# The causal mask of a first attention, written into PSUM by matmuls of 32 rows instead of 128

## The chip, the cores and the metric

The kernel runs on one core of one Trainium2 chip. The metric is device time in microseconds (us); the time before is 1464.79 us, the median of 3 runs (1464.25 to 1464.92). A profile is one further execution, recorded by the hardware profiler.

## What is computed

One transformer block, on 8 sequences (`B`) of 128 tokens (`S`) of width 512:

```
h  = x @ cond_weight[adapter[b]].T             # a weight per sequence, gathered
q, k, v = h @ wq, h @ wk, h @ wv               # 32 query heads of 16, 8 key heads of 16
scores  = q k^T * 16**-0.5, causal: key <= query, else a very negative number
x1 = x + softmax(scores) v @ wo                # the first attention
y  = second attention of x1: 32 heads of 128, RMS norm, RoPE,
     512 cached keys (gathered pages) and 128 own keys, no causal mask
out = x1 + y @ W + b + low-rank terms per sequence
```

Only the causal line is touched by the change. The kernel adds the mask as numbers: it first writes -1e30 where key > query, and 0 elsewhere, into the PSUM banks, and then lets the matmuls of the scores add to them.

## The kernel before, in words

The order of all work is written out by hand: each engine runs its instructions in program order, and a framework only adds the semaphore waits and the rotation of buffers.

**First attention** (lines 662 to 760). A loop over `k` from 0 to 15 takes two steps per sequence (`b = k // 2`, `hb = k % 2`), each with 16 of the 32 heads; `k` = 16 only finishes. In step `k` TensorE runs `scores1(k)` and then the rest of step `k - 1` and the preparation of the next sequence:

- even `k`: `flip_x1(b - 2)` (L477), `condition(b + 1)` (L489), transposes of the probabilities of `k - 1` (`flip_p`, L606), `project_kv(b + 1)` (L519, L523), more transposes, `values1(k - 1)` (L625).
- odd `k`: `out_proj1(b - 1)` (L641), `flip_p`, `project_q(b + 1)` (L503), `flip_p`, `flip_x(b + 2)` (L477), `values1(k - 1)`.

VectorE follows with the negated maxima (`nm`, L572), copies out of PSUM (L497, L514, L612, L632) and the sums (L595, L596), ScalarE with the exponentials (L586), GpSimd with the division (L597) and the gathers of the condition weights (L296, four DMAs a sequence). `values1` uses 32-column groups of the array (128x32 tiles), the score matmuls 32-row groups, everything else in the loop the full array.

`scores1(k)` fills two PSUM tiles of two banks each, so four banks; bank `j` holds four heads by 128 keys for 128 queries. Before, each bank gets one bf16 matmul (L553): stationary `identb` (a 128x128 identity), moving `causal` (the mask four times side by side, 512 columns). Then eight fp32 score matmuls (L563) add to it, `rr` = 0, 1 and `j` = 0 to 3, bank `j` out of rows 32j to 32j+31 of the array. The profile shows each fp32 matmul as two weight loads and two matmuls, so L563 has 16 of each per step and L553 has 4 of each.

**Setting up** (lines 311 to 327). `identb` is a bf16 copy of `ident` (VectorE, L322); GpSimd makes the 128x128 mask (a memset and an affine select in masks.py), VectorE copies it four times to bf16 (L327). On GpSimd these two stand between `gather_w(1)` and `gather_w(2)`.

**Step 1's extra work.** After `values1` of step 1 (`b == 0`), `indices()` and `angles()` (L350 to L390) run on GpSimd and VectorE: the angles of the second attention's tables.

**Buffers.** `tile_a` takes tiles of tag "a" from a ring of 12. The condition weights `cw` (four tiles a sequence) are its first users, and many tiles of the second attention follow. The scores' PSUM tiles come from a ring of two.

**Second attention** (from L767): 64 units of one key head and one sequence, TensorE almost without a gap. The change does not touch it.

Of the kernel before, what the change touches and what calls it, by code (L numbers as in the profile page):

```python
# [10 lines left out]

F32 = mybir.dt.float32
BF16 = mybir.dt.bfloat16
I32 = mybir.dt.int32
AF = mybir.ActivationFunctionType
ALU = mybir.AluOpType
AX = mybir.AxisListType
PSUM = bass.MemoryType.PSUM

P = 128  # L20
# [8 lines left out]
NEG = -1.0e30  # L29
# [12 lines left out]
def block_kernel(  # L42
# [28 lines left out]
    nc = tc.nc  # L71
# [8 lines left out]
    both = ctx.enter_context(tc.tile_pool(name="both", bufs=2))  # L80
# [5 lines left out]
    def one(shape, dtype, name):  # L86
        return const.tile(shape, dtype, tag=name, name=name)

    def tile_a(shape, name):
        return both.tile(shape, F32, tag="a", name=name, bufs=12)  # L90
# [8 lines left out]
    ident = one([P, P], F32, "ident")  # L99
# [177 lines left out]
    with (  # L277
# [40 lines left out]
        ]  # L318
        for v in vpad:
            nc.vector.memset(v[:], 0.0)  # L320
        identb = p1w.tile([P, P], BF16, tag="identb", name="identb")
        nc.vector.tensor_copy(identb[:], ident[:])  # L322
        causal_f = both.tile([P, P], F32, tag="ka", name="causal_f")
        make_causal_mask(nc, causal_f[:], NEG)
        causal = p1w.tile([P, 4, P], BF16, tag="causal", name="causal")
        for n in range(4):
            nc.vector.tensor_copy(causal[:, n, :], causal_f[:])  # L327

        lens = p1w.tile([P, B], I32, tag="lens", name="lens")
        nc.sync.dma_start(out=lens[:], in_=seqlens.unsqueeze(0).to_broadcast([P, B]))  # L330
# [215 lines left out]
        def scores1(k):  # L546
            b, hb = divmod(k, 2)
            h = H[k]
            h["sc"] = [
                p_sc.tile([P, 2, 4 * S], F32, tag="sc", name=f"sc1_{k}_{n}") for n in range(2)  # L550
            ]
            for j in range(4):
                nc.tensor.matmul(  # L553
                    h["sc"][j // 2][:, j % 2, :],
                    identb[:],
                    causal[:].rearrange("p n t -> p (n t)"),
                    start=True,
                    stop=False,
                )
            for rr in range(2):  # L560
                for j in range(4):
                    rows = slice(32 * j, 32 * j + 32)
                    nc.tensor.matmul(  # L563
                        h["sc"][j // 2][:, j % 2, rr * 2 * S : (rr + 1) * 2 * S],
                        qT[b][rows, 2 * hb + rr, :],
                        kbd[b][rows].rearrange("p h t -> p (h t)"),
                        start=False,
                        stop=(rr == 1),
                    )
            h["nm"] = p1.tile([P, 2, 8], F32, tag="nm1", name=f"nm1_{k}")  # L570
            for n in range(2):
                nc.vector.tensor_reduce(  # L572
                    h["nm"][:, n, :],
                    h["sc"][n][:].rearrange("p j (h t) -> p (j h) t", t=S),
                    AX.X,
                    ALU.max,
                    negate=True,
                )
            h["pr"] = []
# [82 lines left out]
        for k in range(2 * B + 1):  # L662
            b, hb = divmod(k, 2)
            more, now, last = b + 1 < B, k < 2 * B, k - 1
            if now:
                scores1(k)
# [415 lines left out]
```

## Time and profile before

| | us |
|---|---|
| median of 3 runs | 1464.79 |
| the profiled execution, its own time | 1463.75 |
| its span (first to last instruction) | 1462.0 |
| PE (TensorE matmul) busy | 1419.5 |
| VectorE (DVE) busy | 931.6 |
| ScalarE (ACT) busy | 653.3 |
| GpSimd (POOL) busy | 553.9 |
| L553, mask matmuls, 64 of them, busy | 16.6 |
| L563, score matmuls, 256 of them, busy | 18.3 |
| first attention, start to about | 248 |

How to read it: the span is the time of the profiled execution between its first and last instruction; what is around it (1.75 us here) is launch and end. Busy times of an engine merge overlapping instructions. PE rows are matmuls, PEld rows weight loads (they overlap the matmuls); matmuls are pipelined, so an instruction's duration is longer than the distance to the next one, and distances between starts say more than durations. A shape such as 32x128 after an engine's name is rows by columns of the array that the instruction uses. The chain of work goes back from the last instruction, at each step to what released it.

### The profile page before, as it was taken

The page shows a single profiled execution, that of the slowest core. Times are in us where ns is not written, and L with a number is a line of the kernel's source. Part 1 is how long each engine was busy: PE and PEld are TensorE (multiplying, and loading weights), DVE is VectorE, ACT ScalarE, POOL GpSimd, SP SyncE. Part 2 cuts the span into 40 slices and gives each one's busy share as a digit, 9 for nine tenths or more (in the row PEclk, how much of TensorE's full clock was granted, in tenths as well). Part 3 has the DMA queues.
Part 4 walks back from the last instruction along what each step waited for, and adds up shares of the span by engine and source line. Part 5 has one row for each costly group of instructions (what it writes and reads, how often), then busy time and mean ns, then how long its engine had stood idle before and what let it go on. Part 6 is the DMA issues. An engine that isn't in the chain of part 4 may idle for free.

```text
span 1462.0 us, 19888 instructions
## 1 busy us (share of the span) xinstructions
PE 1419.5 (97%) x6064; PEld 911.0 (62%) x6064; DVE 931.6 (64%) x2271; ACT 653.3 (45%) x1513; POOL 553.9 (38%) x542
## 2 busy tenths in 40 slices
PE   6899999899999999999999999999999999999997
PEld 5677765466666666666666666666666666566654
DVE  2766665666666667666666676666677656556552
ACT  2545443444444444444444444444444434434430
POOL 4475352433334333344444343333334332333120
PEclk9999999999999999999999999999999999999999
DMA  5232400444444565444445654444466433443331
GB/s 199 66 109 61 174 31 0 121 128 117 117 115 118 152 189 150 119 119 119 119 120 159 192 155 122 123 119 117 117 175 190 129 108 89 115 116 94 80 94 51
DMA packets 155642, 175.00 MB, mean 120 GB/s; under 512 B 94160, under 2 KB 99536, under 8 KB 155536
## 3 DMA queue, kind: packets, MB, share of 16 engines
q1 hardware_dynamic: 140688, 131.77, 32.4%
q0 software_dynamic: 14848, 41.96, 10.1%
q8 instruction: 49, 0.80, 0.2%
q14 instruction: 57, 0.47, 0.1%
HBM read 71.38 MB, written 2.10 MB: 50 GB/s over the span
## 4 chain that ended last, share of the span: by engine, by line
PE 93%; DVE 2%; SPq 2%; DMA 1%; issue 1%; ACT 1%; POOL 1%; DVEq 0%; POOLq 0%
PE op L886 18%; PE sc L830 15%; PE qp L176 15%; PE yp L905 15%; PE kvp L216 7%; PE sc L837 4%; PE att L641 2%; PE qp L503 2%; PE qTp L253 2%; PE hp L489 2%; PE fp L939 2%; PE pT1p L606 2%; PE o L625 1%; SPq L874 1%; PE sc L563 1%; PE sc L553 1%
## 5 line engine op out<-in xcount | busy, mean ns | idle before, releaser
L843 DVE CUSTOM_DVE_ANT_0 pr<-sc,mask,nq 128x640 f32<-128x640 f32 x256 | 225.8, 883 | 151.3 <-PE sc L837 138.1
L853 ACT ACTIVATE pr<-pr,nm 128x640 f32<-128x640 f32 x256 | 211.8, 827 | 190.9 <-DVE nm L843 188.4
L830 PE MATMUL sc<-kT,qT 128*128 128x512 f32 x512 | 263.3, 596 | 1.5 <-ACT kTo L274 1.5
L176 PE MATMUL qp<-wq,x1T 128*128 128x512 f32 x512 | 251.2, 593 | 0.0
L202 POOL TENSOR_TENSOR qa<-qa,qb 128x512 f32<-128x512 f32 x64 | 81.5, 1274 | 438.4 <-DVE sums L820 438.4
L886 PE MATMUL op<-pT,vg 128*128 128x256 f32 x1024 | 242.2, 379 | 2.6 <-DMA pT<-fl 2.1
L905 PE MATMUL yp<-wo,oT 128*128 128x512 f32 x512 | 230.4, 593 | 1.4 <-DVE oT L894 1.4
L886 PEld LDWEIGHTS op<-pT,vg 128*128 128x128 f32 x1024 | 194.2, 190 | 30.5 <-issue 2.3
L821 ACT ACTIVATE pr<-pr,sums 128x640 f32<-128x640 f32 x256 | 208.4, 814 | 0.0
L824 DVE STREAM_TRANSPOSE fl<-pr 128x640 f32<-128x640 f32 x256 | 192.3, 807 | 1.2 <-DMA pT<-fl 0.7
L837 PEld LDWEIGHTS sc<-kTo,qT 128*128 128x128 f32 x512 | 96.8, 190 | 124.9 <-issue 106.3
L905 PEld LDWEIGHTS yp<-wo,oT 128*128 128x128 f32 x512 | 92.4, 190 | 93.7 <-issue 91.8
L159 POOL DMA_INDIRECT kg<-in_k_cache_dram,idx_kv x128 | 131.9, 1031 | 35.3 <-issue 34.9
L159 POOL DMA_INDIRECT vg<-in_v_cache_dram,idx_kv x128 | 127.8, 999 | 36.7 <-issue 36.7
L830 PEld LDWEIGHTS sc<-kT,qT 128*128 128x128 f32 x512 | 88.1, 192 | 79.4 <-issue 72.9
L255 ACT COPY qT<-qTp 128x512 f32<-128x512 f32 x64 | 37.5, 585 | 205.2 <-PE qTp L253 205.2
L216 PEld LDWEIGHTS kvp<-wkv,x1T 128*128 128x128 f32 x512 | 97.3, 190 | 40.5 <-issue 30.4
L216 PE MATMUL kvp<-wkv,x1T 128*128 128x256 f32 x512 | 120.9, 379 | 0.0
L243 POOL TENSOR_TENSOR rs<-ss,minus_half 128x5 f32<-128x5 f32 x64 | 76.5, 1196 | 81.4 <-DVE ss L241 81.4
L176 PEld LDWEIGHTS qp<-wq,x1T 128*128 128x128 f32 x512 | 82.8, 191 | 31.5 <-issue 31.5
L837 PE MATMUL sc<-kTo,qT 128*128 128x128 f32 x512 | 99.3, 276 | 0.0
L597 POOL TENSOR_TENSOR pr<-pr,sums 128x1024 f32<-128x1024 f32 x32 | 60.1, 1897 | 98.5 <-DVE sums L596 91.9
(136 smaller groups left out, 1669.8 us busy)
## 6 DMA issues: line engine op xcount, KB each, us to landing
pT<-fl SPq DMA_DIRECT2D x1024, 80.0 KB
kT<-flk SPq DMA_DIRECT2D x496, 32.0 KB
wq<-in_wq_dram SPq DMA_DIRECT2D x8, 1024.0 KB
wo<-in_wo_dram SPq DMA_DIRECT2D x8, 1024.0 KB
wkv<-in_wkv_dram SPq DMA_DIRECT2D x8, 512.0 KB
xs<-in_x_dram SPq DMA_DIRECT2D x8, 256.0 KB
kg<-in_k_cache_dram,idx_kv POOLq DMA_INDIRECT x128, 3.6
vg<-in_v_cache_dram,idx_kv POOLq DMA_INDIRECT x128, 3.6
```

The source lines that it names most:

```text
L159: nc.gpsimd.indirect_dma_start(out=dst[:, c].rearrange("p n d -> p (n d)"), out_offset=None, in_=src, in_offset=bass.IndirectOffsetOnAxis( ...
L176: nc.tensor.matmul(s["qp"][:].rearrange("p h d -> p (h d)"), x1T[b][:, c, :], weights[g][0][:, c, :], start=(c == 0), stop=(c == KC - 1),)
L202: nc.gpsimd.tensor_tensor(qa[:], qa[:], qb[:], ALU.add)
L216: nc.tensor.matmul(s["kp"][:], x1T[b][:, c, :], weights[g][1][:, c, :], start=(c == 0), stop=(c == KC - 1))
L821: nc.scalar.activation(prs[r][:], prs[r][:], AF.Copy, scale=sums[:, r : r + 1])
L824: nc.vector.transpose(s["flips"][:, :, :, r, :].rearrange("p b c j -> p c b j"), prs[r][:])
L830: nc.tensor.matmul(sc[:, : NBLK * P].rearrange("p (k j) -> p k j", j=32), s["qT"][:, r, :], s["kT"], start=True, stop=True,)
L837: nc.tensor.matmul(sc[:, NBLK * P : NK], s["qT"][:, r, :], s["kTo"][:], start=True, stop=True)
L843: nc.vector.tensor_tensor_reduce(out=pr[:], in0=sc[:, :NK], in1=mask[:], scale=s["nq"][:, r : r + 1], scalar=3.0e38, op0=ALU.add, op1=ALU.min,
L853: nc.scalar.activation(pr[:], pr[:], AF.Exp, bias=nm[:, r : r + 1], scale=-1.0, accum_out=sums[:, r : r + 1],)
L886: nc.tensor.matmul(ops[h][:, : 2 * S], cached(u, "vg", c) if c < NBLK else s["vo"][:], s["pT"][:, :, c, 2 * h : 2 * h + 2, :].rearrange("p ...
L905: nc.tensor.matmul(yp[:], s["oT"][:, r, :], weights[g][2][:, r, :], start=(r == 0), stop=(r == REP - 1))
```

## The change

The mask is no longer one matmul of 128 rows per bank but four matmuls of 32 rows per bank, one for each block `c` of 32 columns (32 keys), and bank `j` uses the rows 32j to 32j+31 of the array, as the score matmuls do. The stationary operand is now the mask (`causal[rows, c, :]`, 32x128: for key 32c+i and query t, -1e30 where t < 32c+i), the moving operand a 32x32 identity repeated for the four heads (`eye32`, 128 columns). A step has 16 mask matmuls and 16 weight loads in place of 4 and 4; the order is `c` outer, `j` inner. The setting up changes with it:

```diff
-        identb = p1w.tile([P, P], BF16, tag="identb", name="identb")
-        nc.vector.tensor_copy(identb[:], ident[:])
-        causal_f = both.tile([P, P], F32, tag="ka", name="causal_f")
-        make_causal_mask(nc, causal_f[:], NEG)
+        eye_f = p1w.tile([P, 32], F32, tag="eye_f", name="eye_f")
+        nc.vector.tensor_reduce(
+            eye_f[:], ident[:].rearrange("p (n r) -> p r n", r=32), AX.X, ALU.add
+        )
+        eye32 = p1w.tile([P, 4, 32], BF16, tag="eye32", name="eye32")
+        nc.vector.tensor_copy(eye32[:], eye_f[:].unsqueeze(1).to_broadcast([P, 4, 32]))
+        row = p1w.tile([P, 1], I32, tag="row", name="row")
+        for n in range(4):
+            nc.gpsimd.iota(
+                row[32 * n : 32 * n + 32, :], pattern=[[0, 1]], base=0, channel_multiplier=1
+            )
+        row_f = p1w.tile([P, 1], F32, tag="row_f", name="row_f")
+        nc.vector.tensor_copy(row_f[:], row[:])
+        ahead = both.tile([P, 4, P], I32, tag="a", name="ahead", bufs=12)
+        nc.gpsimd.iota(ahead[:], pattern=[[-32, 4], [1, P]], base=0, channel_multiplier=0)
+        ahead_f = tile_a([P, 4, P], "ahead_f")
+        nc.vector.tensor_copy(ahead_f[:], ahead[:])
         causal = p1w.tile([P, 4, P], BF16, tag="causal", name="causal")
-        for n in range(4):
-            nc.vector.tensor_copy(causal[:, n, :], causal_f[:])
+        nc.vector.tensor_scalar(causal[:], ahead_f[:], row_f[:], NEG, ALU.is_lt, ALU.mult)
...
-            for j in range(4):
-                nc.tensor.matmul(
-                    h["sc"][j // 2][:, j % 2, :],
-                    identb[:],
-                    causal[:].rearrange("p n t -> p (n t)"),
-                    start=True,
-                    stop=False,
-                )
+            for c in range(4):
+                for j in range(4):
+                    rows = slice(32 * j, 32 * j + 32)
+                    nc.tensor.matmul(
+                        h["sc"][j // 2][:, j % 2, :].rearrange("p (n t) -> p n t", n=4)[
+                            :, :, 32 * c : 32 * c + 32
+                        ],
+                        causal[rows, c, :],
+                        eye32[rows],
+                        start=(c == 0),
+                        stop=False,
+                    )
```

`ahead` and `ahead_f` are two further tiles of the ring of 12 (tag "a"), taken between `gather_w(1)` and `gather_w(2)`. Nothing else is different.

More of the change, by code (lines that the diff above doesn't have):

```diff
@@ L9 @@
 from concourse._compat import with_exitstack
-from concourse.masks import make_causal_mask, make_identity
+from concourse.masks import make_identity
 F32 = mybir.dt.float32
```

## The prediction

> **What bounds the kernel now.** I read the page's busy times and its chain first, then the chain of work stretch by stretch through the first attention, then single starts of L553 and L563 in narrow windows of the timeline.
>
> ```profile
> PE 1419.5 (97%) x6064; PEld 911.0 (62%) x6064; DVE 931.6 (64%) x2271; ACT 653.3 (45%) x1513; POOL 553.9 (38%) x542
> PE 93%; DVE 2%; SPq 2%; DMA 1%; issue 1%; ACT 1%; POOL 1%; DVEq 0%; POOLq 0%
> ```
>
> TensorE is the bound nearly everywhere. The chain of the stretch 112 to 139 us (start, length, what; steps 7 and 8 begin at 113.50 and 126.39) shows it inside one step:
>
> ```profile
> 113.50 0.97 PE sc L553 x4
> 114.47 1.07 PE sc L563 x16
> 115.54 3.63 PE att L641 x8
> ...
> 124.09 0.59 ACT pT L612
> ...
> 126.39 0.97 PE sc L553 x4
> 127.36 1.08 PE sc L563 x16
> 128.43 0.59 PE x1Tp L477 x4
> ```
>
> The mask and the scores are 0.97 + 1.07 = 2.04 us on the chain, and what follows on TensorE starts at once. It is not so everywhere. The chain of 31 to 66 us, where steps 1 and 2 stand:
>
> ```profile
> 44.36 1.90 POOL pr L597
> 46.26 0.06 POOL iota_s L353
> ...
> 47.91 1.40 DVE ang_f L381 x8
> ...
> 54.39 2.26 DVE nm L572 x2
> 56.65 0.61 DVE hT L497
> 57.30 2.07 PE kvp L519 x8
> ```
>
> Here GpSimd (divisions and gathers back to back from 33.82) and then VectorE's angles decide when TensorE goes on at 57.30; it had been idle for 5.0 us. A TensorE that finishes step 1 or 2 sooner only waits longer.
>
> Single starts, from the timeline (start, length from first start to last end):
>
> ```profile
> 101.73 0.60 PE L553 MATMUL sc<-causal,identb 128*128 128x512 bf16 x2
> ```
> ```profile
> 102.70 0.50 PE L563 MATMUL sc<-kbd,qT 32*128 32x256 f32 x4
> ```
> ```profile
> 102.70 0.31 PEld L563 LDWEIGHTS sc<-kbd,qT 32*128 32x128 f32 x8 [0.42 <-issue]
> ```
>
> One L553 takes 379 ns, so the second starts 0.60 - 0.38 = 0.22 after the first: 512 bf16 columns cost 0.216 us each. One L563 of this first round takes 478 ns, so four of them in 0.50 start within 22 ns: the four groups of rows work at once, and even the loads of the next round overlap. The four rounds lie 0.216 apart.
>
> **TensorE per step, before.** Four masks: 4 x 0.216 = 0.86; going over from the column groups of L625 adds 0.10 (0.97; step 1, which follows full-array work, has 0.86 in the chain). Scores: 4 rounds x 0.216 = 0.86, 0.02 within a round, 0.09 for going over from the full array to the row groups (0.309 from the last L553 start to the first L563 start, less 0.216), and 0.10 for first weights that can't be loaded beforehand (478 ns against 374 for later rounds): 1.08. From the first mask start to the start of what follows: 2.04.
>
> **After.** Mask and scores are both in row groups.
> - Going over from L625: the same 0.10, ahead of the first start.
> - Mask: four rounds of four concurrent matmuls of 128 bf16 columns. By L553, 128 columns are 0.216 / 4 = 0.054 us. Starts of rounds at 0, 0.064 (the first bf16 L553 takes 389 ns instead of 379, so a first load shows as 0.01), 0.118, 0.172.
> - First score round: no going over, but its fp32 weights can be loaded only when the last mask round has taken its own, and need 0.104; it starts at 0.172 + 0.104 = 0.276. The others at 0.492, 0.708, 0.924, the last matmul 0.02 later, and the full-array work 0.305 after that, as now (103.474 to 103.779).
> - Together 1.25 us. Saved: 2.04 - 1.25 = 0.79 a step: 0.65 by concurrency, 0.09 by one going-over less, 0.05 by hidden first weights.
>
> No bf16 row-group matmul is in this trace. Bounds for the mask's rounds: below, 0.054 with nothing added (that is my value, since L563's groups overlap completely at the same column rate per pass); above, four loads and matmuls in turn, each at least a weight load of 98 ns (mean of L553's PEld): see the third rival. A gain beyond 0.79 is excluded, as the score rounds and the switches stay.
>
> **The rule against the change.** A step issues 16 loads and 16 matmuls where it issued 4 and 4. The Trainium skill (TensorE: Matmul & The Clock Gate, "Wait — 56ns, not 53.3ns?") says that without hardware decode the sequencer spends about 62 ns on each MATMUL, and that this binds when the array's work is shorter. By it the mask takes 16 x 0.062 = 0.99, the step 0.99 + 0.10 + 0.65 + 0.02 + 0.31 = 2.07, and nothing is won. The row that bears on it is step 0, where TensorE's sequencer waits for VectorE's `qT` with nothing dispatched behind it, and then must dispatch 16 loads and 16 matmuls of L563 before it comes to the wait of L489:
>
> ```profile
> L563 PEldq EVENT_SEMAPHORE  x1: 51/51/51, 26.6 to 26.6; - x1
> ```
> ```profile
> L489 PEldq EVENT_SEMAPHORE  x1: 51/51/51, 26.7 to 26.7; - x1
> ```
>
> The first wait ends at 26.606, the second begins at 26.737: 32 instructions in 0.13 us, 4 ns each. I take the row: dispatch does not bind. The same skill's Part 3 ("Measured speedup vs the span model") gives 3.07 times for four 32-row matmuls of 512 columns, no figure for 128 columns with a load each, and no row here shows it.
>
> **Which steps keep it.** Step 0: L563 waits for `qT` (VectorE L514, 25.82 + 0.69) and starts at 26.66 however early the mask is done: 0. Step 1 saves about 0.7 on TensorE and step 2 0.79, both lost before 57.30: that chain hangs on GpSimd's 33.82, which hangs on VectorE's sums behind step 0. Steps 3 to 15: from 62.47 to 226 us TensorE is busy 161.85 of 163.53 and its waits sum to 1.6 (the longest kind, L477 on ScalarE's copy, 0.24 each, follows TensorE's own transposes and moves with them). 13 steps x 0.79 = 10.3 us. The granted clock is 0.50 from 56 to 62 us, after the idle time, and 0.96 from 62 to 64; TensorE is idle 1.5 us longer before it, which I count at 0, give or take 1 us in when the clock comes back.
>
> What is late next: within a step VectorE and ScalarE start from the scores or from TensorE's results, so they shift along. GpSimd doesn't: its smallest idle stretch per step is 2.1 us (before L597 at 98.05), its results are used 3.6 us later or more, so 0.79 less leaves it covered. The gathers of 200 to 210 us leave 2.9 before L597 at 212.92.
>
> **The setting up: 0.** VectorE loses 0.42 (L322) and 0.66 (L327) and gets a reduction (0.37, L423), a bf16 copy (0.42 at most, L322), a one-column cast (0.15, L360), a 512-column cast (0.43, L770) and a 512-column scalar operation (0.43, L386): 1.8. GpSimd loses 0.52 and gets four small iotas (4 x 0.13, L353) and one of 512 columns (0.57, L769), so `ahead` is there at about 15.5 and `causal` at 16.5. VectorE's next work, L497, comes at 19.42 and the first mask at 25.63, TensorE meanwhile waits for `cw` by DMA and projects. Without that cover it would cost about 1.3.
>
> The two new tiles move the ring by two, so the third and fourth DMAs of `gather_w(2)` reuse slots that `condition(0)` reads: they wait to about 20.2 instead of 17.57, and end at 22.4 on GpSimd. Behind them in GpSimd's queue is L597 at 33.82; their data are used in step 2, at 47.60. `gather_w(3)` now needs `condition(1)` (done 31.6) and goes at 37.72 anyway. Later distances in the ring are 12 as before. SyncE's queue is unchanged: 0.
>
> **Sum.** The span 1462.0 - 10.3 = 1451.7, the profiled execution's own time 1463.75 - 10.3 = 1453.5. The median lies 1.04 above that execution: 1464.79 - 10.3 = 1454.5. About 0.2% (2.9 us) is what this measurement can tell from no change.
>
> **Rivals.**
> - *Half concurrency* (two bf16 row groups at a time[...]): rounds of 0.108, the step 1.25 + 0.17, saved 0.62 x 13 = 8.1: 1456.7. For it: L563 shows 256 columns in 0.216, half the rate at which four bf16 groups would write PSUM. Against: nothing in the trace shows a limit.
> - *Dispatch binds* at 62 ns, or the saving goes into a wait: 2.07 a step: 1465.2, no change. Against: the two waits above and the slack of GpSimd.
> - *Slower: the loads are serial.* If each small bf16 load must end before the next pair goes, a pair costs 98 ns, the mask 1.57, the step 1.57 + 1.08 = 2.65: +0.61 x 13 = 7.9: 1472.7. It decides from (2.04 - 1.08) / 16 = 0.060 us a pair on; by my sum a pair costs 0.014. For it: four times as many loads, each for only 128 columns of work, where L553's hid behind 512. Against: L563's loads overlap by groups.
>
> **Chances.** My forecast 0.76 (1453 to 1456), half concurrency 0.10, no change 0.06, slower 0.08. Range 1452.5 (steps 1 and 2 kept as well would be 1453.0) to 1459; it leaves out the last two. Faster by over 0.2%: 0.86; within: 0.06; slower: 0.08.
>
> **What would show it.** In the profile after: mask matmuls of a step in four rounds about 0.055 apart, their span from first to last start about 0.19 (under 0.06 a pair); no gap of 0.31 between the last mask and the first score; the chain's two pieces together about 1.3 instead of 2.04 in steps 3 to 15; TensorE going on after the angles at 57.3 as before, with a longer idle time; step 16's end and all of the second attention 10 us earlier, with equal length. Wrong if the rounds are longer than 0.11, if TensorE's waits for GpSimd or ScalarE grow by more than 1 us in all, or if the second attention changes its length.

## The result and the profile after

| us | before | after |
|---|---|---|
| median of 6 runs | 1464.74 (1464.11 to 1465.30) | 1454.89 (1452.79 to 1456.03) |
| the profiled execution, its own time | 1463.75 | 1456.03 |
| its span | 1462.0 | 1454.3 |

The ratio is 0.9931, with a 95% interval of 0.9919 to 0.9944: the median came down by 9.85 us. 10.3 was predicted, to 1454.5. The profiled execution of after is the slowest of its six; why is told below.

The page of after, busy times and the chain's shares:

```profile
PE 1408.9 (97%) x6256; PEld 910.0 (63%) x6256; DVE 932.6 (64%) x2271; ACT 653.3 (45%) x1513; POOL 554.4 (38%) x545
PE 91%; DVE 3%; SPq 2%; DMA 1%; issue 1%; ACT 1%; POOL 1%; DVEq 0%; POOLq 0%; ACTq 0%
```

TensorE has 192 matmuls more (16 instead of 4 masks in 16 steps) and is busy 10.6 us less. It still carries the chain. The chain of work of after in the same two steps as before (start, length, what):

```profile
112.50 0.34 PE sc L569 x16
112.83 0.92 PE sc L581 x16
...
122.31 0.59 ACT pT L630
...
124.60 0.34 PE sc L569 x16
124.94 0.92 PE sc L581 x16
125.86 0.59 PE x1Tp L491 x4
```

The two pieces are 0.34 + 0.92 = 1.26 us in both steps where they were 0.97 + 1.07; what lies around them is unchanged (`pT` 0.59, `x1Tp` 0.59). The stretch of steps 1 and 2, again the chain of after:

```profile
46.28 1.90 POOL pr L615
...
49.83 1.40 DVE ang_f L395 x8
...
56.31 2.26 DVE nm L590 x2
...
59.22 2.07 PE kvp L533 x8
```

It is the same chain as before, from GpSimd's division through VectorE's angles, each piece as long as it was, and all of it 1.9 us later. TensorE goes on at 59.22, not at 57.30. In the TensorE timelines of before and then of after, this projection is (start, length, operation, and in brackets the idle time before it with what ended it):

```profile
57.30 2.07 PE L519 MATMUL kvp<-hT,wk_sb 128*128 128x128 f32 x8 [5.00 <-DVE hT L497]
```
```profile
59.22 2.07 PE L533 MATMUL kvp<-hT,wk_sb 128*128 128x128 f32 x8 [6.47 <-DVE hT L511]
```

TensorE waits 1.47 us longer, as much as it won in steps 1 and 2. That all of this is 1.9 us later comes from the start of this execution. Its TensorE timeline to 31 us:

```profile
11.82 0.77 PE L503 MATMUL hp<-xT,cw 128*128 128x128 f32 x2 [5.89 <-DMA cw<-in_cond_w_dram,idx_w]
...
27.64 0.40 PE L569 MATMUL sc<-eye,causal 32*128 32x128 bf16 x16
28.58 1.15 PE L581 MATMUL sc<-kbd,qT 32*128 32x256 f32 x16 [0.54 <-DVE qT L528]
```

TensorE waits 5.89 us for the first condition weights and, in lines left out here, 1.8 more for the later ones (before: 5.82 and 0.9), and the first mask starts at 27.64 instead of 25.62. The longer waits are about half of this. The other half is the clock: in both traces, matmuls in a row on these weights start 0.21 us apart until the first recorded stretch of full clock, and 0.11 apart from then on; that stretch begins at 17.78 before and at 20.54 after. Whether the new setting up does that is what the first experiment asks.

**Step by step.** I measure a step by the distance between the ends of two steps' score blocks (an end is the start of the first TensorE instruction after the scores), read from the single starts in the trace, in us:

| from step to step | before | after | difference |
|---|---|---|---|
| 0 to 1, 1 to 2 | 8.54, 11.32 | 8.03, 10.36 | -1.47 |
| 2 to 3 | 18.70 | 19.63 | +0.93 |
| 3 to 13, five pairs | 5 x (12.89 + 11.69) | 5 x (12.10 + 10.90) | -7.91 |
| 13 to 14 | 12.83 | 12.29 | -0.54 |
| 14 to 15 | 13.79 | 13.00 | -0.79 |
| 0 to 15 in all | 188.1 | 178.3 | -9.78 |

From step 15's end to the second attention it is 32.28 in both, and from its first output projection to the end 1182.25 and 1182.20. So the whole of the saving is in the loop. The profiled execution shows only 7.72 of it, since step 0 ends 1.91 later in it, and a stretch at the start of the second attention is 0.19 longer (last section).

### The profile page after: what moved, and what is told of

It reads as the page before. It is cut to its first block, busy times and chain, and to the rows that moved or that the text cites. A ratio compares the mean times of both kernels' runs of the same rounds, so it can differ in the third digit from the quotient of the medians.

```text
span 1454.3 us, 20275 instructions
## 1 busy us (share of the span) xinstructions
PE 1408.9 (97%) x6256; PEld 910.0 (63%) x6256; DVE 932.6 (64%) x2271; ACT 653.3 (45%) x1513; POOL 554.4 (38%) x545
## 4 chain that ended last, share of the span: by engine, by line
PE 91%; DVE 3%; SPq 2%; DMA 1%; issue 1%; ACT 1%; POOL 1%; DVEq 0%; POOLq 0%; ACTq 0%
PE op L904 18%; PE sc L848 15%; PE qp L176 15%; PE yp L923 15%; PE kvp L216 7%; PE sc L855 4%; PE hp L503 2%; PE qTp L253 2%; PE att L659 2%; PE qp L517 2%; PE fp L957 2%; PE pT1p L624 2%; PE o L643 1%; SPq L892 1%; PE sc L581 1%
```

## The experiments

Each was timed or profiled beside the kernel before on the same chip; ratios are to that.

**1. The new setting up alone.** All new setting-up instructions are issued, and the old ones too; the four old masks are used. (`eye_f` takes its space from another ring.)

```diff
+        eye_f = both.tile([P, 32], F32, tag="kb", name="eye_f")
...
+        nc.vector.tensor_scalar(causal[:], ahead_f[:], row_f[:], NEG, ALU.is_lt, ALU.mult)
...
+        causal4 = p1w.tile([P, 4, P], BF16, tag="causal4", name="causal4")
```

> The whole new setting up (iotas, eye32, the two extra tiles in the ring of 12, the late half of gather_w(2)) and then the old one too, with the old four 128-row mask matmuls. My theory: all of it is covered, so as before, 1464.7 us within 0.6. The rival: the new setting up itself delays the start, as the profiled execution of the changed kernel, whose first mask came 2.0 us later than before, might suggest: 1466 to 1467.

Measured: 1464.46 against 1464.22, ratio 1.0002 (0.9994 to 1.0010). The setting up costs nothing that the time can show, though the interval reaches up to 1.5 us more, the lower part of what the rival asks for. Step 0 ended at 28.77 us in its profile. Over all profiles of this study that end lies between 27.80 and 29.65 with the new setting up, and at 27.74, 28.21 and 29.25 with the old one: the start varies by nearly 2 us either way. A cost of some tenths is not excluded by this.

**2. The order of the loops.** `j` (bank, and group of rows) outside, `c` inside: four matmuls of one group of rows now follow each other.

```diff
-            for c in range(4):
-                for j in range(4):
+            for j in range(4):
+                for c in range(4):
```

> The changed kernel with the two loops exchanged: bank (row group) outer, block of keys inner, so that four matmuls in a row use one row group. My theory: matmuls start in program order and the saving comes from neighbours in different row groups; then the mask takes about 0.66 us from first to last start in place of 0.19, 0.47 more in 13 steps: about 1461. The rival: the array picks freely among the row groups, or the saving comes from somewhere else than concurrency: 1454.9 as with the change.

Measured: 1455.32, ratio 0.9939 (0.9926 to 0.9953). My theory, that a row group's next matmul holds back the others behind it, fell. The TensorE timeline of step 8 in this kernel, and then in after:

```profile
123.90 0.43 PE L569 MATMUL sc<-eye,causal 32*128 32x128 bf16 x16
124.13 1.12 PE L581 MATMUL sc<-kbd,qT 32*128 32x256 f32 x16
```
```profile
124.53 0.40 PE L569 MATMUL sc<-eye,causal 32*128 32x128 bf16 x16
124.77 1.09 PE L581 MATMUL sc<-kbd,qT 32*128 32x256 f32 x16
```

The second column is the time from the first start to the last end. With 0.214 us for one mask matmul, the last of the sixteen starts 0.22 after the first with the exchanged loops, and 0.19 in after. Single starts of step 7, in ns from the first: exchanged 0, 14, 27, 40, then 67, 80, 94, 107; after 0, 3, 7, 10, then 66, 70, 73, 77. In both, a round begins every 56 ns. In the exchanged order the groups follow each other at 13.5 ns, four times the 3.4 ns of after, and in that order there are four pairs of load and matmul from one group to the next. The records don't name the group that a start belongs to. I read them so: pairs are handed to the array at about 3.4 ns each, and each group of rows works through its own, whatever stands ahead of it for another group. One group after the other, at 56 ns a matmul, would have taken some 0.7 us to the last start. The step is 1.28 instead of 1.25.

**3. The new masks in steps 0 to 2 only.**

```diff
+            if k < 3:
+                for c in range(4):
+                    for j in range(4):
...
+            else:
+                for j in range(4):
```

> 32-row masks in steps 0, 1 and 2 only, the old ones in steps 3 to 15, both set up. My theory: nothing is won in these steps, because step 0 waits for qT and the chain through GpSimd and the angles on VectorE sets when TensorE goes on in step 2: 1464.7 within 0.6, with a longer idle time ahead of the projection in step 2. The rival: each step keeps its saving: 1463.2 or less.

Measured: 1464.71 against 1464.22, ratio 1.0001 (0.9993 to 1.0010). The distances of steps 0 to 3 are 8.03, 10.38 and 20.41: the first two are shorter by 1.45 in all, the third is longer by 1.71. In all nine kernels that have the angles in one piece, step 2's projection starts 29.56 to 29.59 after the end of step 0, with any mask. What TensorE wins before the angles, it waits away there.

**4. The new masks twice.** The sixteen mask matmuls are issued a second time and add the mask again, so that a masked score gets -2e30.

```diff
+            for c in range(4):
+                for j in range(4):
...
+                        start=False,
```

> The changed kernel with the 16 mask matmuls of each step issued twice (the second time added, so the mask is twice as negative). My theory: four more rounds of 0.055 a step, 0.22 in 13 steps: 1454.9 + 2.9 = 1457.8. The rival in which a pair of load and matmul costs at least 0.060 by dispatch or by serial loads: 16 x 0.06 x 13 = 12.5 more, 1467.

Measured: 1458.43, ratio 0.9960 (0.9947 to 0.9974). TensorE timeline of step 8:

```profile
123.61 0.40 PE L569 MATMUL sc<-eye,causal 32*128 32x128 bf16 x16
123.84 0.39 PE L581 MATMUL sc<-eye,causal 32*128 32x128 bf16 x16
124.06 1.09 PE L593 MATMUL sc<-kbd,qT 32*128 32x256 f32 x16
```

Sixteen further pairs move the scores by 0.22 us, 14 ns a pair: this is the disputed price by itself. The step is 1.475, or 0.223 more than in after, and the loop from step 0 to 15 takes 2.5 more.

**5. No mask at all.** The mask matmuls are left out, so that this kernel computes the attention without its causal mask.

```diff
-            for c in range(4):
-                for j in range(4):
...
-                        start=False,
+                        start=(rr == 0),
```

> The changed kernel without any mask matmul; the scores' first matmul of each bank starts the sum. It leaves out the causal mask. My theory: what the mask still costs is 1.25 us a step less 0.10 (first weights) + 0.65 (three rounds) + 0.02 + 0.31, so 1.25 - 1.08 = 0.17 in 13 steps, 2.2: 1452.7. If the mask's loads and matmuls cost more than the starts in the trace say: below 1450.

Measured: 1453.97 against 1465.24, ratio 0.9925 (0.9911 to 0.9938). The step is 1.076, 0.176 less than in after, and the loop from step 0's end to step 15's is 2.1 us shorter, as expected; but in the medians only 1.4 of it shows (11.27 less than before here, 9.85 for the change). In its profile the start of the second attention took 1.2 us longer than in after (33.01 instead of 31.79, by the clock; last section), which would cover the difference. What is left of the mask in after is 0.18 us a step.

**6 and 7. Steps 1 and 2 set free.** The angles, 7 us of VectorE in one piece behind step 1, are cut into four parts behind steps 2 to 5, and the tables move to later steps; once with the old masks (7), once with the new (6).

```diff
-                    angles()
+                    angles(1)
...
+                if b in (1, 2):
+                    angles(2 * b - 2)
```

> The kernel before, with the angles cut into four parts of 1.4 to 2 us at the ends of steps 2 to 5 (in buffers that are free then), and the tables two sequences later. VectorE then no longer holds the projection of step 2 back. TensorE's idle 5.0 us and its half clock after it should go, less some 0.3 us for each part: about 5 less than before, 1459 to 1460.

> The same cut angles with the 32-row masks. My theory: steps 1 and 2 now keep their saving too (0.68 and 0.79), so the distance to the same kernel with the old masks is 10.3 + 1.5 = 11.8, about 1448. The rival: these two steps were not covered by that chain, or something else holds them: the distance stays at 9.9 to 10.3, about 1449.5.

Measured: with the old masks 1457.85 against 1465.24, ratio 0.9953 (0.9940 to 0.9967), which is 7.4 less where about 5 was expected: the stretch from step 2 to 3 alone is 7.4 shorter, and with these masks the parts cost nothing (12.89 and 11.69 as before). With the new it is 1448.72, ratio 0.9888 (0.9873 to 0.9903), the fastest of the study. The chain of the latter from 46 us on:

```profile
46.61 0.92 PE sc L592 x16
47.52 3.77 PE hp L514 x32
```

TensorE now carries the chain through step 2, and the stretch from step 2 to 3 is 11.30 with the old masks (18.70 before) and 10.51 with the new. Steps 1 and 2 now keep their saving. But 11.8 (15 steps by 0.79) was expected between the two kernels, 10.5 came in the trace from step 0 to step 15, and 9.1 in the medians (in the two profiles, the start and the second attention's start take 0.85 and 0.5 of it back). VectorE's timeline in step 3 of the kernel with the new masks shows what takes it back:

```profile
57.16 1.37 DVE L398 TENSOR_SCALAR pos<-lens_f,iota_pf 128x8 f32<-128x8 f32 x1
58.56 1.45 DVE L400 TENSOR_SCALAR a_eff<-freq,pos 128x64 f32<-128x64 f32 x8
59.93 2.34 DVE L601 TENSOR_REDUCE nm<-sc 128x8 f32<-128x1024 f32 x2
```

The angles' part (2.8 us) stands in VectorE's queue ahead of the step's maxima (`nm`), whose scores were done at 58. The distances behind parts came out only 0.45, 0.61 and 0.30 shorter than with the old masks, not 0.79: 1.0 in all.

**8. The parts behind the maxima.** Experiment 6, with the parts behind `nm` of steps 2, 4, 6 and 8, and sines and tables later.

```diff
-                if b in (1, 2):
-                    angles(2 * b - 2)
...
+            if hb == 0 and 1 <= b <= 4:
+                angles(b - 1)
```

> The 32-row masks with the four parts of the angles moved from the ends of steps to behind the maxima of steps 2, 4, 6 and 8, where VectorE waits 1.2 to 1.8 us for the next projection, and the sines behind the exponentials of step 9. In the earlier cut they stood ahead of the maxima and took 1.0 back in three steps. My theory: this 1.0 comes back too, about 1447.7. The rival: the parts (1.4 to 2.1 us) only move the delay to the projection's copy: 1448.7 or more.

Measured: 1454.00 against 1467.49, ratio 0.9911 (0.9896 to 0.9926): no better. The later steps did get their 1.0 back (12.10 and 10.90 throughout), but from step 2 to 3 it is 11.97 instead of 10.51. The chain there:

```profile
48.16 2.26 DVE nm L604 x2
...
50.59 1.39 DVE a_eff L400 x8
51.99 0.61 DVE hT L525
```

The first part now delays the copy `hT` that TensorE's projection needs, as the rival has it. And TensorE stood 3.6 us in step 14, a stall that lengthens it by 5.5 (last section); the rest of the loop is 0.5 longer than in experiment 6.

**9. The old masks in sixteen full-array matmuls.** Each mask of 512 columns is issued as four of 128, with 16 loads and 16 matmuls per step as in after, but all on the full array.

```diff
-            for j in range(4):
...
-                    causal[:].rearrange("p n t -> p (n t)"),
+            for n in range(4):
+                for j in range(4):
...
+                        causal[:, n, :],
```

> The kernel before with each 512-column mask matmul cut into four of 128 columns on the full array: 16 loads and 16 matmuls a step, as many and as narrow as in the change, but none beside another. My theory: instructions cost nothing, columns in turn do: 16 x 0.054 = 0.86 as before, with one or two hundredths for switching weights, so 1464.7 to 1465.5. The rival by which a pair costs 0.062 to dispatch: 0.13 more in 13 steps, 1.7: 1466.4 or more. If fewer rows or narrower matmuls by themselves were the saving: well under 1464.

Measured: 1470.47 against 1467.49, ratio 1.0017 (1.0009 to 1.0025). TensorE timeline of a step:

```profile
127.79 1.07 PE L554 MATMUL sc<-causal,identb 128*128 128x128 bf16 x16
```

The sixteen starts are 56 ns apart (with 0.219 us for one, the last comes 0.85 after the first), the whole block 2.07 us a step against 2.04; that makes 0.4 in all. The number of instructions is as in after, and nothing is won: the saving is the concurrency of the groups. The median came out where the rival by dispatch was put (3.0 more; 1.7 or more was asked for), but the trace doesn't bear it out: 0.13 a step would be needed, and the block shows 0.03. The other 2.6 us of the difference in medians are not in these blocks, and stay open; its profile too has the stall of step 14.

**10. The gates' products cut up.** The changed kernel with `merge_gates` of step 12 (2.6 us of VectorE) split: one product there, two behind the maxima of step 13, one at its end.

```diff
-                    merge_gates()
+                    merge_gates((0,))
...
+            if k == 2 * B - 3:
+                merge_gates((1, 2))
...
+                    merge_gates((3,))
```

> The changed kernel with the gates' products of step 12 (2.6 us of VectorE that stand ahead of step 13's maxima) cut up: the selection and the first product stay there (0.9 us), two products follow the maxima of step 13, where VectorE idles 1.27 us for the residual sum, and the last stands at the end of step 13. Theory (in step 13 VectorE, not TensorE, sets the end, which is why that step kept 0.54 of the 0.79): the distance from the end of step 13's scores to the end of step 14's falls from 12.29 to about 12.05 us (the 12.10 of the other steps of that kind less the 0.06 by which it was shorter before), the wait of the values' matmuls for VectorE's copies (0.17) goes, all other distances stay within 0.05, step 14 to 15 included (13.00). Rival (something else of step 13 or 14 costs the 0.25, for instance TensorE's own order there): 12.29 as it was. The one time says nothing on 0.25 us; 1454 to 1457.

Measured by one profiled run: from step 13 to 14 it is 12.04, the wait of the values' matmuls for VectorE's copy is gone, and the theory on step 13 holds. In its timelines, VectorE's maxima of step 13 start 0.74 us after the end of the step's scores by the measure above (1.74 in after), and the values' matmuls run in one piece:

```profile
182.86 2.34 DVE L591 TENSOR_REDUCE nm<-sc 128x8 f32<-128x1024 f32 x2
```
```profile
191.07 1.91 PE L644 MATMUL o<-pT,vpad 128*32 128x256 f32 x16
```

Its one time, 1460.97 beside 1469.06, says nothing on that, and that all other distances stay was not borne out: the step 14 stall was there again (18.43 instead of 13.00), and from step 3 to 4, where nothing was changed, VectorE was late once (12.87 instead of 12.10).

## Why the prediction was right, point by point

**The step on TensorE: 2.04 to 1.25.** Measured 1.25 in every step from 2 to 15. Its parts were nearly right. The mask's rounds were to start at 0, 0.064, 0.118 and 0.172; they started at 0, 0.066, 0.122 and 0.178, so a round is 0.056. The first score round was put at 0.276, because its fp32 weights were to be loaded unhidden, 0.05 beyond a mask round; it came at 0.233, a mask round's distance, so nothing was paid there. The second came 0.272 later, not 0.216, and the 0.056 was paid at that place. The total is off by 0.003. The end of the list was right by this compensation, not by its own terms. (The 2.04 before was put together from distances of ends: between the two starts that are named lies the going back to the full array, 0.09, and not the going over from L625, 0.10. The saving is not touched by this.)

**The concurrency (0.65 of the 0.79).** Shown from two sides: sixteen more pairs on the groups cost 0.22 (experiment 4), sixteen pairs on the full array 0.85 from first to last start (experiment 9). Half concurrency would have doubled the former.

**The rule against the change.** At the 62 ns that the Trainium skill (TensorE: Matmul & The Clock Gate, "Wait — 56ns, not 53.3ns?") gives for each MATMUL with hardware decode off, experiment 4 would have added 0.99 us a step, 15 in all by this estimate, and lost everything. It added 0.22 a step, 2.5 to the loop, and 3.1 to the median of experiment 2 on the same chip. The row of step 0 (32 instructions in 0.13 us, 4 ns each, so 8 a pair) was the right one to take; the exchanged loops show less still, 3.4 ns from pair to pair.

**Steps 0 to 2 keep nothing.** Right: experiment 3 has the time of before, and TensorE's wait ahead of step 2's projection is 1.47 longer in after (1.5 was predicted). From step 0 to 3 after has only 0.54 less, though step 3's own 0.79 is in it. The missing 0.25 is the clock, which the prediction counted at 0, give or take 1 us in when it comes back. By the clock rows of the traces it came back 4.85 us after the start of that projection before, and 5.69 after it in after. The same 2 us of the two, seen from there (before, then after; the last but two is the granted clock):

```profile
62.00:64.00 2.00, 1.96 (x20) 0.96 (x18) 0.58 (x2) 1.74 (x5) 1.84 (x2) 0.96 0.00 0
```
```profile
64.00:66.00 2.00, 1.94 (x19) 0.87 (x18) 0.50 (x2) 1.59 (x4) 1.84 (x2) 0.77 0.00 0
```

Experiment 3, with the old mask in step 3, had its clock back after 5.67, as late as after. From the projection to the end of step 3 it took 9.24; after took 8.45, just 0.79 less, and before, with the earlier clock, 9.00. Whether the change itself delays the clock is open: the return lay at 4.42 to 5.30 in the three profiles with the old masks in steps 1 and 2 and the angles in one piece, and at 4.96 to 6.03 in the six with the new.

**Steps 3 to 15 keep 13 x 0.79.** Step 3 did, once the clock is allowed for, and eleven others did. The one that was mis-sized is step 13, which kept 0.54. I had listed what is late next within a step as following the scores, and had checked GpSimd's slack; of VectorE I had only said that it shifts along. In step 13 it doesn't. VectorE in the timeline of after:

```profile
181.68 1.09 PE L581 MATMUL sc<-kbd,qT 32*128 32x256 f32 x16
...
182.29 2.22 DVE L443 TENSOR_TENSOR gs<-gc,sel 128x256 f32<-128x256 f32 x4
...
184.44 1.21 DVE L590 TENSOR_REDUCE nm<-sc 128x8 f32<-128x1024 f32 x1
```

The gates' products start from an earlier result of TensorE and stand ahead of the maxima, which start at 184.44 though the scores ended at 182.77. Late maxima make the last copy of probabilities late, and TensorE waits for it (timeline of after):

```profile
192.75 1.05 PE L643 MATMUL o<-pT,vpad 128*32 128x256 f32 x10 [0.17 <-DVE pT L630]
```

Three kernels with a mask of 0.18 us less, 0.03 more and 0.22 more than after (experiments 5, 2 and 4) all have 12.28 or 12.29 from step 13 to 14: there the mask is no longer on the path. Cutting the products up gave the 0.25 back (experiment 10).

**The setting up at 0, the gathers at 0.** Right within what the time shows (1.0002, 0.9994 to 1.0010); some tenths stay open. `causal` was there at 16.63 (16.5 predicted). Of the two gathers that were to wait, one did (1.41 us, to 20.87).

**GpSimd's slack.** Right: from 62 to 217 us TensorE's waits in after are the same two as before (1.2 for ScalarE's `pT`, 0.4 for VectorE's) and the 0.2 of step 13; none is for GpSimd.

**The sum.** 10.3 predicted, 9.85 in the medians, 9.78 in the loop of the two traces. There 0.25 is step 13 and 0.24 the clock behind the angles. For the profiled execution I had written 1453.5, and it took 1456.03: 1.9 of the 2.5 is its start, 0.5 the loop, 0.2 the clock in the second attention.

**The signs.** Rounds 0.056 (0.055 named), first to last mask 0.19, the two pieces 1.26, the second attention as long as before: all seen. TensorE "going on at 57.3 as before" was wrong as a number, 59.22: what I should have named is its distance to the end of step 0, 29.56 before and 29.57 after. The second attention was to come 10 us earlier; in this execution it came 7.9 earlier, by its late start.

**The rivals.** Half concurrency (1456.7) and serial loads (1472.7) fell with experiments 2, 4 and 9, no change by dispatch (1465.2) with experiment 4.

## What to carry to other kernels

Small matmuls whose contraction fits 32 rows were worth moving to the row groups that their neighbours already use: the gain is the columns streamed at once plus the change of mode that is saved, and the extra instructions cost little here (3.4 ns from pair to pair, 14 ns for a further pair in all). Count what a step on the path saves only where TensorE carries the path through the whole step; where another engine's chain ends the stretch, here VectorE's angles, the saving is waited away. Moving that chain won 0.5% by itself and 1.1% together with the masks, which won 0.7% alone: steps 1 and 2 then kept their saving in the trace, but other steps lost most of it again, and the medians don't show it. Ask of every engine, in every step that is unlike the others, what stands in its queue between the earlier release and the scores: one piece of 2.6 us in one step of sixteen was enough to take away a third of that step's saving.

## What the runs showed of the hardware that was not expected

- **Row groups run by themselves.** By the reading given with experiment 2, starts interleave over the groups even when four matmuls of one group stand in a row in the program (0, 14, 27, 40 and again 67 ns).
- **First fp32 weights after bf16 in the same groups** do not cost at one place: the first round comes 0.055 us after the last mask round, the second 0.272 after the first, the later ones 0.216 apart.
- **The start varies.** Step 0 ended between 27.74 and 29.65 us. The arrival of the first condition weights doesn't order this: they were used from 10.83 on in experiment 7 with the old masks, and from 11.73 in before, but step 0 ended at 28.21 there and at 27.74 here. The clock goes with it better: where the first recorded stretch of full clock begins by 18.0 us, step 0 ended by 28.16 (three profiles), and where it begins after 19.9, at 28.86 or later (four).
- **The clock after an idle stretch.** At the start of the second attention TensorE idles for some us (4.79 of 8 busy in the line below), and the granted clock then falls to a half: for 3.41 us before and for 6.83 after, which makes 0.79 and 0.60 of the 8 us that hold it. What it costs goes by the moment of its return. In before, after and experiment 5 full clock came back 18.82, 19.20 and 21.68 us after the second attention's start, and the stretch from there to the first output projection took 31.60, 31.79 and 33.01, half a us more for each us. The other nine profiles lie in the same order. The stretch of after (its length, busy time of TensorE, its weight loads, VectorE, ScalarE and GpSimd with counts, then the granted clock, the DMA share and GB/s):

```profile
251.00:259.00 8.00, 4.79 (x14) 2.81 (x15) 4.30 (x12) 2.06 (x7) 4.67 (x6) 0.60 0.37 97
```

- **A stall in step 14, left open.** In the profiles of experiments 8, 9 and 10, on two chips where the kernel before took 1467.5 and 1469.1, step 14 is 4.6 to 5.5 us longer than elsewhere, with old masks and new. The chain of experiment 9, and VectorE's timeline in it:

```profile
204.40 5.18 PE aeff L439 x24
209.59 2.79 issue
212.37 2.79 PE aeff L439 x8
```
```profile
211.90 0.42 DVE L446 COPY a_eff<-aeff 128x256 f32<-128x256 f32 x1 [5.21 <-remote]
```

TensorE goes on 0.05 after VectorE's second copy `a_eff` ends, and that copy had waited 5.2 us for something that the trace does not name, while GpSimd issued its gathers. The copy came 0.2 after the last of these had been issued; in experiment 8 it was 0.1, in experiment 10 it was 1.7. In before and after the same copies waited 1.3 for TensorE. What held VectorE there was not tried; that the kernel before has the stall on these chips too would fit its times, but no profile of it was taken there.
